# Four graph layers on one core: a planner that counts TensorE's instructions, attention summed by key tile, and checks and turns begun beside the LSTM

## The chip, the cores and the metric

The kernel runs on one core of one Trainium2 chip. Its time is device time in microseconds, the median of three runs. The program is one launch, and its input is packed on the host without arithmetic.

## The reference, cut to what matters

There are 32 graphs of 512 nodes with 128 features each, and one symmetric 0/1 adjacency for each graph. Four layers follow each other. Every one of them normalizes its input, cuts it at zero and adds its result to the residual.

```python
# layer 0: attention over neighbours
v, q, k = relu(h @ Wv.T + bv), relu(h @ Wq.T + bq), relu(h @ Wk.T + bk)
scores = einsum('bih,bjh->bij', q, k)
s = clip(scores * mask, 0.0, CLAMP_HI) - NEG_PENALTY * (1.0 - mask)
x = x + softmax(s, axis=2) @ v

# layer 1: an LSTM over the last 128 nodes makes weights of each graph
dyn = conv1d(h[:, -128:, :]) + conv_b
lw = lstm(dyn)                                # 128 steps, one after the other
x = x + sigmoid((A_norm @ h) @ lw)            # A_norm = D^-1/2 (A + I) D^-1/2

# layer 2: four times
src_agg = (adj / rownorm) @ (nodes @ ws + bs)
dst_agg = (adj.T / colnorm) @ (nodes @ wd + bd)
out = tanh(concat([src_agg, nodes @ wn + bn, dst_agg]) @ wu + bu)

# layer 3
g = adj @ (h @ W.T) + bias
x = x + where(g >= 0, g, a * g)
```

## The kernel before

The program has three stages. In the first (`pass_1`, one call for each batch) it computes keys, values and the attention of a batch's last 128 nodes, which is all that the LSTM needs, and stores keys, queries and values in DRAM.

In the second stage the LSTM runs. It handles all 32 batches in one step, so there are 128 steps in a row. A step goes from TensorE (`f_z`, L1234) to ScalarE (`f_th`, L1260), VectorE (`f_cu`, L1266, and `f_th`, L1267), ScalarE (`f_tcn`, L1274), VectorE (`f_h`, L1278, and a transpose into `f_seq`, L1279), and back to TensorE. Beside it runs `pass_2`: for each batch the attention of the first 384 nodes. For each of four key tiles there is a product of scores (`f_s`, L1325), an exponential (`f_e`, L1328) and a product with the mask (L1329). Then the values are summed (`f_po`, L1334): for each of three query tiles over the four key tiles. All these products, like those of the LSTM, are cut into four quarters of 32 columns (`quarters`); the planner calls such work tiled and counts a switch to other work as 0.28 or 0.1 us. For batches 0 to 21 (`EARLY`), `pass_2` also makes layer 1's neighbour sums (`f_pg`, L1419) and stores them. Batches 26 and 27 (`FIRST`) keep their adjacency `a`, its squared copy `ar` and their rows in SBUF, so that their later turns begin without loads. Batches 28 to 31 come late (`LATE`).

In the third stage (`rest`) each batch takes a turn: layer 1's end (`f_pl`, L1477), the four layers of layer 2 (`f_py` L1523, `f_pa` L1419 for the sums over neighbours and L1534 for a node's own part, `f_y` L1402 and L1403, the scaling of `f_pa` by the degrees at L1530, `f_n` L1538), and layer 3. The order of turns is 26, 27, then 0 to 25, then 28 to 31.

Each turn also checks that the adjacency equals its transpose, because the program uses that. GpSimd writes `ar` to DRAM as bf16 (`f_das`, L1491), a transposing transfer issued by SyncE brings it back turned (`f_aT`, L1493), and VectorE compares it with `a` in two passes (`f_junk`, L1496), with the count in `viol`. If a check had failed, a general program would run instead.

What stands where is decided by a planner in the kernel (`Plan.run`). Each operation has a rank, the time that it is expected to take, the tiles that it reads and writes, and a gap by which its result comes later. The planner plays the program through. At each step it takes the operation that can start first, by rank among those ready, and reserves buffers (`BUFS`) and PSUM banks. Ranks below 1000 are the LSTM's. Ranks from 20,000 are `pass_2`, ranks from 30,000 (`plan.last`) are `rest`, and the first two turns' main work is moved up beside the LSTM by `SOON`. The instructions are then issued on each engine in the order of the planned start times. Each engine works through its list in order. `hold_back` ties a load that belongs beside the LSTM to an LSTM step on VectorE that ends before its planned start, so that it is not issued earlier.

Of the kernel before, what the change touches and what calls it, by code (L numbers as in the profile page):

```python
# [8 lines left out]
FP = mybir.dt.float32  # L9
# [4 lines left out]
P = 128  # L14
# [503 lines left out]
class Op:  # L518
    __slots__ = ("engines", "rank", "no", "deps", "cells", "waits", "ready", "end", "engine", "start", "next", "gap", "tiled", "patience")


class Plan:
# [14 lines left out]
    SWITCH = (0.28, 0.1)  # L537

# [30 lines left out]
    def op(self, engines, rank, reads=(), writes=(), after=(), gap=0.0, tiled=False):  # L569

        o = Op()
        o.engines, o.rank, o.no, o.gap = engines, rank, len(self.ops), gap
        o.tiled = tiled
        o.patience = 0.15
        deps = set(after)
        cells = []
        for acc, is_write in [(a, False) for a in reads] + [(a, True) for a in writes]:
            c, part = acc if isinstance(acc, tuple) else (acc, None)
            if c not in cells:
                cells.append(c)  # L580
            for key, (ws, rs) in c.parts.items():
                if part is None or key is None or key == part:
                    deps.update(ws)
                    if is_write:
                        deps.update(rs)
            mine = c.parts.setdefault(part, ([], []))
            if is_write:
                c.parts[part] = ([o], [])
            else:
                mine[1].append(o)  # L590
        deps.discard(o)
        o.deps = list(deps)
        o.cells = [c for c in cells if c.pool is not None]
        for c in o.cells:
            c.left += 1
        self.ops.append(o)
        return o

    def hold_back(self, tc, made, o, steps):

        while len(steps) > 1 and steps[1][0] + self.ACROSS["SP"] < o.start:
            steps.pop(0)
        if self.spared <= o.rank < self.last and steps[0][0] + self.ACROSS["SP"] < o.start:
            tc.add_manual_dep(made.ins, steps[0][1].name, mybir.DependencyInfo(
                mybir.DependencyClass.Sync, mybir.DependencyReason.DATA), reason="issued in step with the LSTM")

    def run(self, tc, queues):
# [89 lines left out]
        tiled = False  # L697
        by_rank = sorted((o for o in ops if o.rank >= 10_000 and o not in apart), key=lambda o: -o.rank)
        while done < len(ops):
            best = None  # L700
            for e, cands in pools.items():
                first = None
                held = expected.get(e)
                for rank, no, o in cands:
                    r = room(o)
                    if r is None:
                        continue
                    if r:
                        r += self.HOP
                    s = max(free[e], o.ready[e], r)  # L710
                    if e == "PE" and o.tiled != tiled and rank >= self.spared:
                        s = max(s, free[e] + self.SWITCH[o.tiled])
                    if len(o.engines) > 1:
                        mine = s + o.engines[e][0]
                        if any(max(free[x], o.ready[x], r) + o.engines[x][0] < mine - 1e-9 for x in o.engines if x != e):
                            continue
                    if rank < self.URGENT:
                        held = s
                    elif held is not None and s < held < s + o.engines[e][0] - o.patience:
                        continue  # L720
# [14 lines left out]
            if e == "PE":  # L735
                tiled = o.tiled
            if o.rank < self.URGENT:
                foresee(o)
# [23 lines left out]
        steps = []  # L762
        with tc.manual_schedule(engines=queues):
# [8 lines left out]
def symmetric(ctx, tc, x, adj, weights, cols, rows, lstm_b, prelu_a, out, fail):  # L772
# [20 lines left out]
    FIRST = [B - LATE - 2 + k for k in range(2)]  # L793
    EARLY = range(22)
# [104 lines left out]
    viol = const.tile([P, B, 2], FP, name="f_viol")  # L899
# [320 lines left out]
    def lstm():  # L1220
# [20 lines left out]
        PE(2_000, MANY * T_STEP, lambda z=z: first(z), [], [z], after=conv_ops, tiled=True)  # L1241
        coming, after_th = z, None
        for t in range(T):
# [11 lines left out]
            if t or coming is not None:  # L1255
                ahead = 0.0 if coming is None else T_STEP
                PE(R, ahead + (T_STEP if t else 0.0), step, [], ([z] if t else []) + ([coming] if coming else []),
                   after=last, gap=-ahead, tiled=True)
# [30 lines left out]
    def pass_2(b):  # L1289
# [26 lines left out]
        PE(R, t_mm(NR), lambda: quarters(lambda p: nc.tensor.matmul(pq.t[p], w[:, W_Q, p], hT.t, start=True, stop=True)), [hT], [pq], tiled=True)  # L1316
# [5 lines left out]
        es = []  # L1322
        for j in range(NT):
            s = bank(f"f_s_{b}_{j}", (P, NR), whole=False)
            PE(R, t_mm(NR), lambda s=s, j=j: quarters(lambda p: nc.tensor.matmul(  # L1325
                s.t[p], keys.t[:, j * P + p.start : j * P + p.stop], q.t, start=True, stop=True)), [keys, q], [s], tiled=True)
# [3 lines left out]
            es.append(e)  # L1330
        po = bank(f"f_po_{b}", (P, L, P + 1), whole=False)
        for t in range(L):
            for j in range(NT):
                PE(R, t_mm(P), lambda t=t, j=j: quarters(lambda p: nc.tensor.matmul(  # L1334
                    po.t[p, t, :], es[j].t[:, t * P + p.start : t * P + p.stop], v.t[:, j, :], start=(j == 0), stop=(j == NT - 1))),
                    [es[j], v], [po], tiled=True)
# [5 lines left out]
        if whole and not early:  # L1342
            begun[b] = a, xc, ar, deg
        else:
# [23 lines left out]
    def squares(rank, b, a, name):  # L1368
# [6 lines left out]
        return ar, deg  # L1375

# [38 lines left out]
    def aggregate(rank, parts, ar, pg):  # L1415
# [9 lines left out]
        if rank < plan_rest:  # L1425
            last = PE(rank, 8 * t_r(N), both, [parts, ar], [pg])
# [6 lines left out]
    def rest(b, turn, lw_after):  # L1433
# [54 lines left out]


        das = plan.fixed(dram.tile([N, N], BF, tag=f"s{b}", name=f"f_das_{b}"))  # L1490
        POOL(R + 2, 1.4, lambda: nc.gpsimd.dma_start(das.t.rearrange("(t p) j -> p t j", p=P), f32(ar.t)), [ar], [das], gap=6.0)  # L1491
        aT = new("y", (P, NT, N), f"f_aT_{b}", BF)
        plan.op({"SP": (3.0, lambda: nc.sync.dma_start_transpose(out=aT.t, in_=das.t))}, R + 2, [das], [aT], gap=4.0)  # L1493
        for k in range(2):
            def differ(k=k):
                nc.vector.scalar_tensor_tensor(junk, flat(a.t[:, 2 * k : 2 * k + 2, :]), 1.0, flat(aT.t[:, 2 * k : 2 * k + 2, :]),  # L1496
                                               OP.mult, OP.not_equal, accum_out=viol[:, b, k : k + 1])
            differ_ops.append(DVE(R + 2, 1.2, differ, [a, aT], []))


# [91 lines left out]
    def counted():  # L1592
# [10 lines left out]
        def places():  # L1603
            nc.vector.tensor_reduce(bad[:, 1:2], flat(viol), AX.X, OP.add)
# [11 lines left out]
    sum_ops, differ_ops, late = [], [], []  # L1616
# [8 lines left out]
    for k, b in enumerate(FIRST + [b for b in range(B) if b not in FIRST]):  # L1625
        rest(b, k, end)
# [87 lines left out]
```

## Time and profile before

| what | us |
|---|---|
| median of 3 runs | 1301.07 |
| lowest, highest | 1301.03, 1301.52 |
| the profiled execution | 1305.92 |
| span of its profile, first to last instruction | 1304.0 |
| first `f_z` product to last | 181.8 to 503.3 |
| share of the chain that ended last that is TensorE's | 85% |

The profile is of one execution, and its span is a little shorter than the time, which also has the start and the end of the launch. "Idle before" a group of instructions is time in which their engine did nothing just before them, with what ended it; "issue" means that no other engine's signal ended it. The profile records each fp32 product as two matmuls with a weight load each.

This is the share of the chain by line. The attention's products and the LSTM's stand on it as well as the graph layers':

```profile
PE f_pa L1419 17%; PE f_py L1523 14%; PE f_pa L1534 14%; PE f_pg L1419 8%; PE f_po L1334 5%; PE f_s L1325 5%; PE f_z L1234 4%; PE f_pk L1141 2%; PE f_pol L1184 2%; PE f_pv L1157 2%; PE f_p L1575 2%; PE f_sl L1174 2%; PE f_pl L1477 2%; PE f_pd L1209 2%; PE f_pq L1316 1%
```

### The profile page before, as it was taken

How to read it: one execution, taken by the hardware profiler on the slowest of the kernel's cores; microseconds unless marked ns; L12 is line 12 of the kernel's file. 1: busy time of each engine (PE TensorE's matmuls, PEld its weight loads, DVE VectorE, ACT ScalarE, POOL GpSimd, SP SyncE). 2: the span in 40 equal slices, each digit the busy share in tenths (PEclk: the TensorE clock that was granted, in tenths of full speed). 3: DMA queues.
4: the chain of work that ended last, by engine and by line, in shares of the span. 5: the costliest groups of instructions: out<-in, count | busy, mean ns of one | idle time of the engine just before them, and what ended most of it. 6: DMA issues, size and time to landing. Idle time of an engine off the chain costs nothing.

```text
span 1304.0 us, 32965 instructions
## 1 busy us (share of the span) xinstructions
PE 1268.1 (97%) x12087; PEld 976.6 (75%) x12087; DVE 990.3 (76%) x3284; ACT 830.2 (64%) x2079; POOL 389.8 (30%) x733
## 2 busy tenths in 40 slices
PE   9999999998999999899999999999999999999997
PEld 6888876666766677677778787787777877877774
DVE  7989878877978787587667677676776787787754
ACT  5666667777777554577566676666766665675423
POOL 4654533222222133232213223132231322332000
PEclk9999999999999999899999999999999999999998
DMA  8888888887746655889476667666676366673311
GB/s 259 270 275 285 265 271 273 257 262 252 246 140 215 209 182 139 198 191 243 103 152 156 155 163 163 154 159 154 162 160 144 86 136 145 139 170 65 50 33 35
DMA packets 300699, 232.03 MB, mean 178 GB/s; under 512 B 140656, under 2 KB 246128, under 8 KB 300528
## 3 DMA queue, kind: packets, MB, share of 16 engines
q1 hardware_dynamic: 283632, 213.06, 58.4%
q0 software_dynamic: 16896, 16.78, 8.4%
q8 instruction: 97, 1.59, 0.5%
q14 instruction: 74, 0.61, 0.2%
HBM read 136.19 MB, written 62.13 MB: 152 GB/s over the span
## 4 chain that ended last, share of the span: by engine, by line
PE 85%; DVE 5%; DMA 3%; ACT 2%; issue 2%; POOL 1%; SPq 0%; ACTq 0%; DVEq 0%
PE f_pa L1419 17%; PE f_py L1523 14%; PE f_pa L1534 14%; PE f_pg L1419 8%; PE f_po L1334 5%; PE f_s L1325 5%; PE f_z L1234 4%; PE f_pk L1141 2%; PE f_pol L1184 2%; PE f_pv L1157 2%; PE f_p L1575 2%; PE f_sl L1174 2%; PE f_pl L1477 2%; PE f_pd L1209 2%; PE f_pq L1316 1%
## 5 line engine op out<-in xcount | busy, mean ns | idle before, releaser
L1419 PE MATMUL f_pa<-f_ar,f_y 128*128 128x512 f32 x1024 | 295.6, 426 | 0.7 <-ACT f_y L1402 0.7
L1419 PEld LDWEIGHTS f_pa<-f_ar,f_y 128*128 128x128 f32 x1024 | 189.4, 188 | 72.1 <-issue 37.3
L1523 PE MATMUL f_py<-f_wf,f_n 128*128 128x128 f32 x1280 | 175.0, 276 | 0.0
L1523 PEld LDWEIGHTS f_py<-f_wf,f_n 128*128 128x128 f32 x1280 | 165.4, 192 | 9.3 <-ACT f_n L1538 1.4
L1534 PE MATMUL f_pa<-f_n,f_wf 128*128 128x512 f32 x320 | 153.0, 593 | 0.3 <-DVE f_pa L1530 0.3
L1538 ACT ACTIVATE f_n<-f_pa,f_bcol 128x512 f32<-128x512 f32 x128 | 88.3, 690 | 93.5 <-PE f_pa L1534 93.4
L1373 ACT ACTIVATE f_ar<-f_a 128x512 fp32r<-128x512 f32 x216 | 133.6, 621 | 5.3 <-PE f_pg L1419 3.1
L1402 ACT CAST f_y<-f_py 128x512 fp32r<-128x512 f32 x128 | 74.7, 584 | 93.7 <-PE f_py L1523 88.4
L1491 POOL DMA_DIRECT2D f_das<-f_ar x32 | 27.8, 868 | 354.0 <-ACT f_ar L1373 284.5
L1334 PE MATMUL f_po<-f_v,f_e 128*32 128x129 f32 x3072 | 106.3, 274 | 6.0 <-issue 5.9
L1334 PEld LDWEIGHTS f_po<-f_v,f_e 128*32 128x32 f32 x3072 | 89.3, 110 | 20.4 <-issue 13.2
L1403 DVE TENSOR_TENSOR f_y<-f_py,f_y 128x512 fp32r<-128x512 f32 x128 | 87.4, 686 | 22.0 <-ACT f_y L1402 21.8
L1325 PE MATMUL f_s<-f_q,f_k 128*32 128x384 f32 x1024 | 100.6, 490 | 0.0
L1530 DVE TENSOR_TENSOR f_pa<-f_pa,f_inv 128x512 f32<-128x512 f32 x128 | 86.6, 693 | 16.5 <-PE f_pa L1419 16.1
L1234 PE MATMUL f_z<-f_w,f_seq 128*32 128x128 f32 x2040 | 85.1, 277 | 10.6 <-DVE f_seq L1279 4.2
L1534 PEld LDWEIGHTS f_pa<-f_n,f_wf 128*128 128x128 f32 x320 | 57.9, 190 | 47.1 <-issue 37.7
L1234 PEld LDWEIGHTS f_z<-f_w,f_seq 128*32 128x32 f32 x2040 | 55.4, 109 | 48.1 <-issue 11.4
L1496 DVE SCALAR_TENSOR_TENSOR f_junk<-f_a,f_aT 128x1024 bf16<-128x1024 f32 x64 | 78.1, 1221 | 7.1 <-DMA f_aT<-f_das 6.1
L1419 PE MATMUL f_pg<-f_ar,f_xp_d 128*128 128x512 f32 x256 | 75.3, 417 | 0.3 <-DVE f_xp_d L1411 0.2
L1523 PE MATMUL f_py<-f_wf,f_T_c 128*128 128x128 f32 x448 | 72.9, 275 | 0.0
L1328 ACT ACTIVATE f_e<-f_s 128x384 f32<-128x384 f32 x128 | 60.8, 484 | 17.7 <-PE f_s L1325 9.9
L1096 DVE COPY f_hl_d<-f_n 128x1024 uint16<-128x1024 uint16 x28 | 19.4, 694 | 68.8 <-ACT f_n L1538 68.8
(197 smaller groups left out, 2756.8 us busy)
## 6 DMA issues: line engine op xcount, KB each, us to landing
f_a<-in_adj_dram SPq DMA_DIRECT2D x30, 1024.0 KB
f_a<-in_adj_dram SPq DMA_DIRECT2D x96, 256.0 KB
f_das<-f_ar POOLq DMA_DIRECT2D x32, 512.0 KB, 4.8
f_dkq<-f_kh SPq DMA_DIRECT2D x32, 448.0 KB
f_dv<-f_v SPq DMA_DIRECT2D x32, 258.0 KB
f_v<-f_dv SPq DMA_DIRECT2D x32, 258.0 KB
f_x<-in_x_dram SPq DMA_DIRECT2D x32, 256.0 KB
f_al<-in_adj_dram SPq DMA_DIRECT2D x32, 256.0 KB
```

The lines of the kernel that those rows point to most:

```text
L1234: nc.tensor.matmul(z.t[part, k, :, :], h, w[:, m : m + 4, part], start=False, stop=True, skip_group_check=True)
L1325: PE(R, t_mm(NR), lambda s=s, j=j: quarters(lambda p: nc.tensor.matmul(s.t[p], keys.t[:, j * P + p.start : j * P + p.stop], q.t, start=Tru ...
L1334: PE(R, t_mm(P), lambda t=t, j=j: quarters(lambda p: nc.tensor.matmul(po.t[p, t, :], es[j].t[:, t * P + p.start : t * P + p.stop], v.t[:, ...
L1373: ACT(rank, 0.62, lambda t=t: nc.scalar.activation(ar.t[:, t, :], a.t[:, t, :], AF.Square, accum_out=deg.t[:, t : t + 1]), [(a, t)], [(ar, ...
L1402: ACT(rank, t_act(N), lambda: nc.scalar.copy(parts.t[:, :, 0, :], src.t), [src], [(parts, 0)])
L1403: DVE(rank, t_dve(N), lambda: nc.vector.tensor_sub(parts.t[:, :, 1, :], src.t, f32(parts.t[:, :, 0, :])), [src, (parts, 0)], [(parts, 1)])
L1419: nc.tensor.matmul(pg.t, parts.t[:, j, k, :], ar.t[:, j, :], start=(k == 0 and j == 0), stop=(k == 1 and j == NT - 1))
L1496: nc.vector.scalar_tensor_tensor(junk, flat(a.t[:, 2 * k : 2 * k + 2, :]), 1.0, flat(aT.t[:, 2 * k : 2 * k + 2, :]), OP.mult, OP.not_equal ...
L1523: nc.tensor.matmul(py.t[:, j, :], nodes[n].t[:, bass.ts(j, P)], wf[:, W_F[i] + c, 0, :], start=False, stop=(c == nch - 1), skip_group_chec ...
L1530: before = DVE(R, t_dve(N), lambda pa=pa: nc.vector.tensor_mul(pa.t, pa.t, inv_row.t), [inv_row], [pa])
L1534: nc.tensor.matmul(pa.t, wf[:, W_F[i] + c, 1, :], nodes[n].t, start=False, stop=(c == nch - 1), skip_group_check=True)
L1538: ACT(R, 0.57, lambda pa=pa, n=n, i=i: nc.scalar.activation(n.t, pa.t, AF.Tanh, bias=bcol[:, i : i + 1]), [pa], [n])
```

## The change

It has four parts.

1. The planner counts TensorE's instructions. Each operation gets a `count`, 8 if nothing is said. `supplied` gives the time from which TensorE can have an operation's instructions: 5 us (`FETCH`) after the instruction that stands 264 (`AHEAD`) before them was taken, and 32 (`KEEP`) fewer are available to work that is not the LSTM's while the LSTM runs. Nothing waits in the program for this; it alters which operation is chosen next.
2. Attention in `pass_2` adds to `f_po` as soon as a key tile's weights are there: for each key tile over the three query tiles, where it was for each query tile over the key tiles. One `start` flag is set for the bank, on the first of these products.
3. The check becomes a function, `turned_back`. For batches 26 and 27 it is called in `pass_2`, beside the LSTM, with VectorE's part in four pieces of one tile each. For the others it stays in the turn with two pieces.
4. Batches 22 and 23 (`NEXT`) take the third and fourth turn. Their adjacency is loaded in four pieces. `hold_back` now covers every load planned to start before the LSTM's end, those of later ranks too.

```diff
+    AHEAD, FETCH, KEEP = 264, 5.0, 32
...
-        if self.spared <= o.rank < self.last and steps[0][0] + self.ACROSS["SP"] < o.start:
+        if self.spared <= o.rank and o.start < self.left_at and steps[0][0] + self.ACROSS["SP"] < o.start:
...
+        taken, at_time = [0], [0.0]
+
+        def supplied(o):
+
+            n = taken[-1] + o.count + (self.KEEP if o.rank >= self.URGENT and self.left else 0) - self.AHEAD
+            if n <= 0:
+                return 0.0
+            k = bisect.bisect_left(taken, n)
+            return at_time[k] + self.FETCH - o.engines["PE"][0]
...
-                    if e == "PE" and o.tiled != tiled and rank >= self.spared:
-                        s = max(s, free[e] + self.SWITCH[o.tiled])
+                    if e == "PE":
+                        s = max(s, supplied(o))
+                        if o.tiled != tiled and rank >= self.spared:
+                            s = max(s, free[e] + self.SWITCH[o.tiled])
...
+                taken.append(taken[-1] + o.count)
+                at_time.append(o.end)
...
+        self.left_at = max(o.end for o in order if o.rank < self.URGENT)
...
+    NEXT = [22, 23]
...
-        es = []
+        po = bank(f"f_po_{b}", (P, L, P + 1), whole=False)
         for j in range(NT):
...
-            es.append(e)
-        po = bank(f"f_po_{b}", (P, L, P + 1), whole=False)
-        for t in range(L):
-            for j in range(NT):
-                PE(R, t_mm(P), lambda t=t, j=j: quarters(lambda p: nc.tensor.matmul(
-                    po.t[p, t, :], es[j].t[:, t * P + p.start : t * P + p.stop], v.t[:, j, :], start=(j == 0), stop=(j == NT - 1))),
-                    [es[j], v], [po], tiled=True)
+            for t in range(L):
+                PE(R, t_mm(P), lambda e=e, t=t, j=j: quarters(lambda p: nc.tensor.matmul(
+                    po.t[p, t, :], e.t[:, t * P + p.start : t * P + p.stop], v.t[:, j, :], start=(j == 0 and t == 0),
+                    stop=(j == NT - 1), skip_group_check=True)), [e, v], [po], tiled=True, count=16)
...
         if whole and not early:
             begun[b] = a, xc, ar, deg
+            turned_back(R + 5, b, a, ar, NT)
...
+    def turned_back(rank, b, a, ar, pieces):
+
+        das = plan.fixed(dram.tile([N, N], BF, tag=f"s{b}", name=f"f_das_{b}"))
+        POOL(rank, 1.4, lambda: nc.gpsimd.dma_start(das.t.rearrange("(t p) j -> p t j", p=P), f32(ar.t)), [ar], [das], gap=6.0)
+        aT = new("y", (P, NT, N), f"f_aT_{b}", BF)
+        plan.op({"SP": (3.0, lambda: nc.sync.dma_start_transpose(out=aT.t, in_=das.t))}, rank, [das], [aT], gap=8.0 if b in NEXT else 4.0)
+        n = NT // pieces
+        for k in range(pieces):
+            at = differs[0]
+            differs[0] += 1
+
+            def differ(k=k, at=at):
+                nc.vector.scalar_tensor_tensor(junk[:, : n * N], flat(a.t[:, n * k : n * (k + 1), :]), 1.0, flat(aT.t[:, n * k : n * (k + 1), :]),
+                                               OP.mult, OP.not_equal, accum_out=viol[:, at : at + 1])
+            differ_ops.append(DVE(rank, 0.08 + 0.56 * n, differ, [a, aT], []))
...
-            DMA(R, 1024, lambda: nc.sync.dma_start(a.t, adj[b].rearrange("(t p) j -> p t j", p=P)), [], [a])
+            if b in NEXT:
+                for t in range(NT):
+                    DMA(R, 256, lambda t=t: nc.sync.dma_start(a.t[:, t, :], adj[b, t * P : (t + 1) * P, :]), [], [(a, t)], gap=LANDED)
+            else:
+                DMA(R, 1024, lambda: nc.sync.dma_start(a.t, adj[b].rearrange("(t p) j -> p t j", p=P)), [], [a])
...
+        if b not in begun:
+            turned_back(R + 2, b, a, ar, 2)
...
-    for k, b in enumerate(FIRST + [b for b in range(B) if b not in FIRST]):
+    for k, b in enumerate(FIRST + NEXT + [b for b in range(B) if b not in FIRST + NEXT]):
         rest(b, k, end)
```

Counts of 16 are given to the tiled products and to `f_pg` beside the LSTM, 64 to the LSTM's first products and 16 or 32 to a step's.

More of the change, by code (lines that the diff above doesn't have):

```diff
@@ L518 @@
 class Op:
-    __slots__ = ("engines", "rank", "no", "deps", "cells", "waits", "ready", "end", "engine", "start", "next", "gap", "tiled", "patience")
+    __slots__ = ("engines", "rank", "no", "deps", "cells", "waits", "ready", "end", "engine", "start", "next", "gap", "tiled", "patience", "count")
 class Plan:
@@ L567, in fixed, with op @@
         return c
-    def op(self, engines, rank, reads=(), writes=(), after=(), gap=0.0, tiled=False):
+    def op(self, engines, rank, reads=(), writes=(), after=(), gap=0.0, tiled=False, count=8):
         o = Op()
@@ L574, in op @@
         o.patience = 0.15
+        o.count = count
         deps = set(after)
@@ L898, in symmetric @@
     nc.vector.memset(neg_half, -0.5)
-    viol = const.tile([P, B, 2], FP, name="f_viol")
+    viol = const.tile([P, 2 * B + 2 * len(FIRST)], FP, name="f_viol")
     rinv = const.tile([P, B, NT], FP, name="f_rinv")
@@ L1240, in lstm @@
         z = biased(0)
-        PE(2_000, MANY * T_STEP, lambda z=z: first(z), [], [z], after=conv_ops, tiled=True)
+        PE(2_000, MANY * T_STEP, lambda z=z: first(z), [], [z], after=conv_ops, tiled=True, count=64)
         coming, after_th = z, None
@@ L1257, in lstm @@
                 PE(R, ahead + (T_STEP if t else 0.0), step, [], ([z] if t else []) + ([coming] if coming else []),
-                   after=last, gap=-ahead, tiled=True)
+                   after=last, gap=-ahead, tiled=True, count=16 * ((t > 0) + (coming is not None)))
             th, after_th = after_th or new("th", (P, 5, TURN), f"f_th_{t}"), new("th", (P, 5, TURN), f"f_th_{t + 1}")
@@ L1315, in pass_2 @@
         pq = bank(f"f_pq_{b}", (P, NR), whole=False)
-        PE(R, t_mm(NR), lambda: quarters(lambda p: nc.tensor.matmul(pq.t[p], w[:, W_Q, p], hT.t, start=True, stop=True)), [hT], [pq], tiled=True)
+        PE(R, t_mm(NR), lambda: quarters(lambda p: nc.tensor.matmul(pq.t[p], w[:, W_Q, p], hT.t, start=True, stop=True)), [hT], [pq], tiled=True, count=16)
         q = new("xn", (P, NR), f"f_q_{b}")
@@ L1325, in pass_2 @@
             PE(R, t_mm(NR), lambda s=s, j=j: quarters(lambda p: nc.tensor.matmul(
-                s.t[p], keys.t[:, j * P + p.start : j * P + p.stop], q.t, start=True, stop=True)), [keys, q], [s], tiled=True)
+                s.t[p], keys.t[:, j * P + p.start : j * P + p.stop], q.t, start=True, stop=True)), [keys, q], [s], tiled=True, count=16)
             e = new(f"n{j}" if j < 3 else "y", (P, NR), f"f_e_{b}_{j}")
@@ L1425, in aggregate @@
         if rank < plan_rest:
-            last = PE(rank, 8 * t_r(N), both, [parts, ar], [pg])
+            last = PE(rank, 8 * t_r(N), both, [parts, ar], [pg], count=16)
             last.patience = PATIENCE
@@ L1486, in rest @@
         xn = ln_full(R, xc, f"c2{b}", moved)
[L1490 to L1498, printed above, removed]
+        if b not in begun:
+            turned_back(R + 2, b, a, ar, 2)
         turned_d = new("dt", (P, TURN), f"f_dT_{b}")
@@ L1603, in places @@
         def places():
-            nc.vector.tensor_reduce(bad[:, 1:2], flat(viol), AX.X, OP.add)
+            nc.vector.tensor_reduce(bad[:, 1:2], viol, AX.X, OP.add)
             nc.vector.tensor_add(bad[:, 0:1], bad[:, 0:1], bad[:, 1:2])
@@ L1614, in counted @@
         PE(R, 0.1, read, [], [], after=[said] + late)
-    sum_ops, differ_ops, late = [], [], []
+    sum_ops, differ_ops, late, differs = [], [], [], [0]
     junk = const.tile([P, 2 * N], BF, name="f_junk")
```

## The prediction

> **What bounds the kernel now.** I read the page first (shares of busy time, the slices, the fetch queue), then busy time by stretch with cuts where the stages change, then TensorE's waits, then the timeline at the two places where TensorE is idle longest.
>
> ```profile
> PE 1268.1 (97%) x12087; PEld 976.6 (75%) x12087; DVE 990.3 (76%) x3284; ACT 830.2 (64%) x2079; POOL 389.8 (30%) x733
> ...
> PEclk9999999999999999899999999999999999999998
> ...
> q8 instruction: 97, 1.59, 0.5%
> ```
>
> TensorE is busy for 97% of the span, no other engine over 76%. The stretches (length, busy time of PE, PEld, DVE, ACT and POOL, granted clock, DMA share, GB/s) say where the other 3% is:
>
> ```profile
> 0.00:181.80 181.80, 177.69 (x1420) 148.83 (x1420) 153.74 (x686) 114.87 (x230) 96.41 (x248) 1.00 0.86 272
> 181.80:450.00 268.20, 254.68 (x5190) 176.43 (x5183) 219.51 (x900) 192.78 (x681) 66.78 (x129) 1.00 0.75 234
> 450.00:503.40 53.40, 50.30 (x1204) 38.82 (x1203) 45.67 (x201) 30.91 (x112) 16.55 (x33) 0.97 0.55 172
> 503.40:526.60 23.20, 17.82 (x169) 14.92 (x161) 14.11 (x59) 8.02 (x22) 7.60 (x12) 0.97 0.77 165
> 526.60:540.00 13.40, 13.40 (x59) 9.95 (x60) 7.91 (x14) 9.03 (x22) 2.98 (x5) 0.79 0.69 203
> 540.00:1165.00 625.00, 624.64 (x3382) 489.19 (x3381) 461.96 (x1203) 413.92 (x899) 176.93 (x277) 1.00 0.69 155
> 1165.00:1304.00 139.00, 129.55 (x687) 98.46 (x685) 87.37 (x226) 60.66 (x116) 22.56 (x32) 0.97 0.24 53
> ```
>
> From 540 to 1165 us TensorE lacks 0.36 us: there only less matmul work could help. It is idle 16.6 us beside the LSTM (181.8 to 503.4: 13.5 + 3.1), 5.4 us at the seam after it (503.4 to 526.6), 4.1 us in the first stage and 9.5 us in the last. A lower clock adds 53.4 x 0.03 = 1.6 us and 13.4 x 0.21 = 2.8 us. TensorE's waits (total us, times, longest) name the causes, and the timeline shows the two worst:
>
> ```profile
> PE f_po L1334 <- issue: 5.9, 5, 2.3
> PE f_z L1234 <- DVE f_seq L1279: 4.2, 8, 1.1
> PE f_pa L1534 <- DVE f_sh_c L1076: 3.8, 1, 3.8
> PE f_z L1234 <- ACT f_ar L1373: 2.1, 4, 1.5
> PE f_z L1234 <- issue: 1.5, 2, 1.1
> ```
>
> ```profile
> 470.16 0.94 PE L1334 MATMUL f_po<-f_v,f_e 128*32 128x129 f32 x25
> ...
> 473.37 1.50 PE L1334 MATMUL f_po<-f_v,f_e 128*32 128x129 f32 x36 [2.27 <-issue]
> ...
> 475.55 0.25 ACT L1260 ACTIVATE f_th<-f_z 128x96 f32<-128x96 f32 x1 [4.27 <-PE f_z L1234]
> ```
>
> ```profile
> 524.69 1.22 DVE L1496 SCALAR_TENSOR_TENSOR f_junk<-f_a,f_aT 128x1024 bf16<-128x1024 f32 x1 [3.35 <-DMA f_aT<-f_das]
> ...
> 526.44 0.15 DVE L1076 SCALAR_TENSOR_TENSOR f_sh_c<-f_mv_c,f_rs_c 128x4 f32<-128x4 f32 x1
> ```
>
> ```profile
> 526.59 2.08 PE L1534 MATMUL f_pa<-f_hT_c,f_wf 128*128 128x512 f32 x2 [3.78 <-DVE f_sh_c L1076]
> ```
>
> "Issue" in the midst of one row of like matmuls is a wait for nothing that another engine does: TensorE had no instructions. In the last two (VectorE's, then TensorE's timeline) VectorE stands 3.35 us at the check f_junk, for the turned adjacency; the scaling of f_pa by the degrees, which the next TensorE product needs, stands behind it, and TensorE idles 3.78 us.
>
> [...] 1.59 MB in 97 packets is 16.4 KB each, and TensorE's 2 x 12087 recorded instructions over 97 are 249. [...] 7.4 us (5.9 + 1.5) are waits for issue. [...] here all 32 f_aT are on SyncE's queue and hold it 1.3 to 5.2 us, median 2.25.
>
> **The change, part by part.** The matmuls are the same in number and shape, but for two.
>
> *Fetch.* One block is 128 recorded matmuls and their 128 weight loads. The chain of waits has 72 f_po in 1.99 us, 27.6 ns each: a block of nothing but f_po lasts 3.5 us; with f_s (24 in 1.94 us, 81 ns) it lasts longer. Before the stalls at 352, 445, 461 and 473 us the last 128 matmuls had taken 4.2, 4.3, 3.6 and 3.6 us; before the one at 417 us 6.2, so density is most of the cause, not all. I priced the order in which each built program's TensorE instructions stand with such durations (f_z 27.8 ns, f_pg 229 ns from later rows): of all starting points beside the LSTM the next 264 instructions hold under 4.0 us of work in 8% before and in none after, under 4.75 us in 26% before and 2% after; the least after is 4.5 us. Five LSTM steps before have no other TensorE work between them, none after. So of 7.4 us I take off 6.5, leaving 0.9 (bounds 3 and 7.4), and 1.5 of the 1.6 us of clock after the 2.3 us stall. That attention sums by key tile is what lets f_s and f_po mix in short pieces; its own product count stays 3072 records. It also holds a PSUM bank for f_po from the first key tile on: bounds 0 to +2 us; I take 0, as the LSTM's two f_z banks and this one leave five of eight.
>
> *Marking products.* The two f_marks matmuls beside the LSTM (L963) are not in the new order: 2 x 0.39 = -0.8 us.
>
> *Seam.* The checks of the two batches begun early go from the seam to steps 111 to 118 of VectorE's LSTM order, and four turns instead of two are ready when the LSTM ends. The wait at 524.69 us has no place any more. Of the 5.4 us idle (3.78, 0.92, 0.67) I keep 1.5 us for the first products, which wait for ScalarE and VectorE whichever turn comes first: -3.9; with them goes most of the clock loss, -2.3 of 2.8. Bounds: nothing, and -8.2. What is late next are the checks of batches 22 and 23, whose transfers get more planned time (gap 8 for 4). Each issues a GpSimd write (to landing 4.7 to 8.0 us), a SyncE transpose and two VectorE passes; their 1.22 us passes are hidden as now, since TensorE lacks nothing after 540 us.
>
> *Added beside the LSTM.* Eight check pieces of 512 columns, about half of 1.22 us plus 0.08, some 0.7 each: 5.6 us of VectorE, which is busy 82% there (265.2 of 321.6). A step's own VectorE work stands behind a piece, and TensorE's f_z behind that; other products fill some: +1.0 (0 to +3). Behind the same two waits on f_aT stand LSTM steps, not graph layers (a rival below). The two transposes hold SyncE 2.25 us each; loads queued behind them are due at least 3.8 us ahead: 0 (0 to +1.5). Two adjacencies come in four pieces each, now held to LSTM steps: the DMA share there is 0.75, so 0. Three more f_pg visits: eight f_pg take 2.04 us beside the LSTM and 1.83 us later, so 3 x 0.2 = +0.6.
>
> *Not changed.* f_z waits for other engines 8.2 us (4.2, 2.1 and five small ones); I leave them (bounds -5 and +3). The two extra f_pg of 1.83 us for batches 22 and 23 move from late turns to the seam: 0. The last 90 us of the two TensorE orders are the same row by row, so the tail's 9.5 us stay.
>
> **Sum.** -6.5 - 1.5 - 0.8 - 3.9 - 2.3 + 1.0 + 0.6 = -13.4 us on the profiled execution, 1305.92 us with a span of 1304.0 and 1.9 around it. The runs' median is 1301.07, 4.85 less; some of the waits may be longer under the profiler, so I give back 1.5: -11.9, or **1289.2 us**.
>
> **Rivals.** (1) *The seam's gap is only replaced*: four turns at once want GpSimd's norms (f_dinv L1453 alone 1.72 us each) and the DMA queues, 0.98 and 1.01 busy from 580 to 620 us; TensorE waits for a layer norm as it did for the check. For it: such a wait for f_aT came again at 609 us. Against: there it cost TensorE only 0.34 us. Only fetch and marks count: -6.5 - 1.5 - 0.8 + 1.6 + 1.5 = -5.7, 1295.4. (2) *The evener order also ends the waits of f_z*: fewer steps start late, 8.2 falls to about 3: -17.1, 1284. (3) *The fetch waits are a matter of DMA traffic, not of density* (the stall at 417 us speaks for it, the other four against): the seam alone, -0.8 - 3.9 - 2.3 + 1.6 + 1.5 = -3.9, 1297.2. (4) *Slower: VectorE stands at the checks beside the LSTM*, at steps 111 and 116, until f_aT lands; each us is a us of the LSTM, since every step passes VectorE. The slowest f_das and f_aT here took 8.0 and 8.05 us, 16 together against 14.4 planned (1.4, 6, 3 and 4): 1.7 us a check. It decides from 6 us a check on and is slower by over 0.2% from 7.3; at 8 each, 1301.1 - 11.9 + 16 = 1305.
>
> **How the numbers follow.** Forecast 0.53, (1) 0.22, (2) 0.13, (3) 0.08, (4) 0.04. The forecast's own bounds reach about 1284 to 1295; with (1) and most of (2) the range is 1282 to 1297. No change means within 0.2%, 2.6 us, about what a measurement here can tell: faster is below 1298.5, which takes in all but (4) and some of (3).
>
> **What would show it.** Right: TensorE's waits for issue under 1.5 us in all, clock 1.00 from 450 us to the LSTM's end, the span from the first to the last f_z at 310 to 315 us instead of 321.5, idle under 2 us at the seam, no f_marks product after the start, f_junk's first start before the last f_z. Wrong: issue still above 4 us (3), a new idle of over 3 us soon after the last f_z (1), or a VectorE wait on f_aT of several us among the LSTM's steps (4).

## The result, and the profile after

| | before | after |
|---|---|---|
| median of 6 runs, us | 1302.87 | 1289.8 |
| lowest, highest | 1301.03, 1305.94 | 1287.1, 1293.02 |
| the profiled execution, its span | 1305.92, 1304.0 | 1290.13, 1288.3 |
| first to last `f_z` product | 181.8 to 503.3 | 179.0 to 495.9 |

The ratio of after to before is 0.9901, interval 0.9878 to 0.9923: faster by 1.0%. Of the six runs of before, three are those of the table above (1301.0 to 1301.5 us); the three taken beside after took 1304.2 to 1305.9. The page of after, with the same lines as the prediction showed of before:

```profile
PE 1259.9 (98%) x12085; PEld 971.5 (75%) x12085; DVE 985.2 (76%) x3279; ACT 834.1 (65%) x2092; POOL 386.9 (30%) x733
...
PEclk9999999999999999999999999999999999999999
...
q8 instruction: 97, 1.59, 0.5%
```

The clock row shows no dip any more. Busy time by stretch of after (length, busy PE, PEld, DVE, ACT, POOL, granted clock, DMA share, GB/s), cut where its own stages change:

```profile
0.00:179.00 179.00, 173.86 (x1380) 147.33 (x1384) 150.77 (x672) 113.66 (x226) 94.74 (x245) 1.00 0.87 272
179.00:450.00 271.00, 259.10 (x5289) 181.16 (x5283) 224.24 (x925) 201.88 (x715) 69.24 (x136) 1.00 0.77 242
450.00:495.90 45.90, 44.38 (x969) 30.95 (x961) 40.28 (x172) 30.45 (x110) 15.38 (x33) 1.00 0.86 241
495.90:520.00 24.10, 23.91 (x348) 20.97 (x346) 22.53 (x92) 15.77 (x45) 14.11 (x22) 1.00 0.68 150
520.00:540.00 20.00, 19.91 (x143) 15.24 (x142) 17.04 (x45) 16.02 (x36) 5.84 (x11) 1.00 0.92 216
540.00:1150.00 610.00, 610.00 (x3307) 477.65 (x3306) 444.13 (x1152) 395.46 (x849) 167.50 (x258) 1.00 0.69 150
1150.00:1288.30 138.30, 128.75 (x684) 98.16 (x682) 86.22 (x225) 60.86 (x116) 20.06 (x31) 0.98 0.23 53
```

Read as length less PE busy: beside the LSTM TensorE is idle 11.9 + 1.5 = 13.4 us (16.6 before), at the seam after it 0.19 + 0.09 = 0.3 us (5.4 before), at a clock of 1.00 where before had 0.79. The last stretch has its 9.5 us still. What remains beside the LSTM, by TensorE's waits (total us, times, longest), and the longest wait for issue in the timeline:

```profile
PE f_z L1252 <- issue: 5.0, 3, 2.0
PE f_z L1252 <- DVE f_seq L1297: 2.9, 7, 1.1
PE f_z L1252 <- ACT f_ar L1389: 2.1, 4, 1.5
```

```profile
408.91 0.61 PE L1252 MATMUL f_z<-f_w,f_seq 128*32 128x128 f32 x14
411.48 0.27 PE L1252 MATMUL f_z<-f_w,f_seq 128*32 128x128 f32 x1 [1.95 <-issue]
```

The reader is to see two things. The wait for a layer norm at the seam is gone from the list. The waits for issue are not: they fell from 7.4 us to 5.0 (three waits), and now they stand within a row of `f_z`, on the LSTM's own path, where the profile shows no other engine late.

The span fell by 15.7 us. Idle time gives 35.9 - 28.4 = 7.5 of it: 3.2 beside the LSTM and 5.1 at the seam, with 1.0 more in the first stage and small changes elsewhere. Busy time gives 8.2: 4.4 were the lower clock (1.6 + 2.8, as the prediction worked them out), 0.8 the two marking products, and 3.0 are spread over many groups and not assigned.

### The profile page after: what moved, and what is told of

Read it like the earlier page. It is cut to its first block, busy times and chain, and to the rows that moved or that the text cites. A ratio compares the mean times of both kernels' runs of the same rounds, so it can differ in the third digit from the quotient of the medians.

```text
span 1288.3 us, 33017 instructions
## 1 busy us (share of the span) xinstructions
PE 1259.9 (98%) x12085; PEld 971.5 (75%) x12085; DVE 985.2 (76%) x3279; ACT 834.1 (65%) x2092; POOL 386.9 (30%) x733
## 4 chain that ended last, share of the span: by engine, by line
PE 86%; DVE 7%; ACT 2%; DMA 2%; POOL 1%; issue 1%; DVEq 0%; ACTq 0%; SPq 0%; POOLq 0%
PE f_pa L1451 18%; PE f_py L1548 15%; PE f_pa L1559 15%; PE f_pg L1451 8%; PE f_s L1343 5%; PE f_z L1252 4%; PE f_po L1349 4%; PE f_p L1600 2%; PE f_pk L1159 2%; PE f_pv L1175 2%; PE f_pl L1513 2%; PE f_pol L1202 2%; PE f_sl L1192 2%; PE f_pd L1227 1%; PE f_pq L1334 1%
## 5 line engine op out<-in xcount | busy, mean ns | idle before, releaser
L1451 PE MATMUL f_pa<-f_ar,f_y 128*128 128x512 f32 x1024 | 299.3, 429 | 0.0
L1252 PE MATMUL f_z<-f_w,f_seq 128*32 128x128 f32 x2040 | 83.6, 276 | 12.6 <-issue 5.0
L1252 PEld LDWEIGHTS f_z<-f_w,f_seq 128*32 128x32 f32 x2040 | 53.0, 109 | 48.7 <-issue 16.4
L1405 DVE SCALAR_TENSOR_TENSOR f_junk<-f_a,f_aT 128x1024 bf16<-128x1024 f32 (+1 forms) x68 | 78.5, 1154 | 4.7 <-DMA f_aT<-f_das 3.7
L1114 DVE COPY f_hl_d<-f_n 128x1024 uint16<-128x1024 uint16 x28 | 19.4, 693 | 75.9 <-ACT f_n L1563 75.9
L1086 ACT ACTIVATE f_xn_c<-f_x,f_sh_c,f_rs_c 128x128 f32<-128x128 f32 x140 | 59.1, 486 | 18.9 <-DVE f_sh_c L1094 18.5
```

Of the source, the lines that this page charges most:

```text
L1252: nc.tensor.matmul(z.t[part, k, :, :], h, w[:, m : m + 4, part], start=False, stop=True, skip_group_check=True)
L1405: nc.vector.scalar_tensor_tensor(junk[:, : n * N], flat(a.t[:, n * k : n * (k + 1), :]), 1.0, flat(aT.t[:, n * k : n * (k + 1), :]), OP.mu ...
L1451: nc.tensor.matmul(pg.t, parts.t[:, j, k, :], ar.t[:, j, :], start=(k == 0 and j == 0), stop=(k == 1 and j == NT - 1))
```

## The experiments

A kernel with one part undone is also planned anew, and the order of everything beside the LSTM changes with it. So each run was read twice: by its ratio to before, and by two stages of its trace. The table is the summary. The measured times of e1, e2, e3, e5, e6 and e7 lie outside every band that their expectations had set, so the traces, not the totals, carry what follows. The idle times are length less PE busy; "issue + f_seq" is the sum of TensorE's waits for these two from 170 to 520 us (to 600 in e9 to e12).

| kernel | us | ratio to before (95%) | idle beside LSTM | issue + f_seq | idle in the 60 us after last f_z |
|---|---|---|---|---|---|
| before | 1302.87 | 1 | 16.6 | 7.4 + 4.2 | 5.4 |
| after | 1289.8 | 0.9901 (0.9878, 0.9923) | 13.4 | 5.0 + 2.9 | 0.3 |
| e1 no counting | 1299.91 | 0.9968 (0.9952, 0.9984) | 17.7 | 3.8 + 7.0 | 1.4 |
| e2 checks back | 1319.09 | 1.0104 (1.007, 1.0138) | 11.8 | 4.4 + 3.7 | 6.0 |
| e3 no NEXT | 1299.38 | 0.9942 (0.9917, 0.9966) | 15.0 | 4.7 + 2.7 | 3.4 |
| e4 old sum | 1290.53 | 0.9886 (0.9849, 0.9922) | 12.9 | 0.2 + 7.2 | 0.3 |
| e5 two checks left out | 1298.94 | 0.9957 (0.9936, 0.9977) | 11.0 | 2.5 + 4.7 | 3.3 |
| e6 counting and sum only | 1308.34 | 1.0031 (1.0019, 1.0043) | 12.7 | 5.7 + 2.5 | 7.7 |
| e7 seam parts only | 1304.12 | 0.9985 (0.9967, 1.0003) | 24.8 | 8.6 + 10.8 | 2.9 |
| e9 e7, two comparisons left out | 1301.05 | 0.9983 (0.9962, 1.0003) | 18.0 | 6.9 + 5.1 | 0.5 |
| e10 old hold_back | 1291.86 | 0.9899 (0.988, 0.9917) | 14.3 | 5.3 + 3.0 | 0.1 |
| e11 refill 4.8 us | 1291.46 | 0.9908 (0.9883, 0.9934) | 12.7 | 2.5 + 6.5 | 0.8 |
| e12 refill 5.2 us | 1300.1 | 0.9957 (0.9942, 0.9973) | 15.0 | 1.4 + 9.0 | 2.8 |

**The scale of what a total can tell: e11 and e12.** They differ from after, and from each other, in one number of the planner.

```diff
-    AHEAD, FETCH, KEEP = 264, 5.0, 32
+    AHEAD, FETCH, KEEP = 264, 4.8, 32      (e12: 5.2)
```

> The changed kernel with the planner's refill time 4.8 us instead of 5.0: a control. The order beside the LSTM is drawn anew, the work packed there is nearly the same (1.5 us more before the last f_z, by my pricing of the order), 9.7% instead of 4.9% of the starting points have under 5 us of work. If differences of 8 to 18 us between the variants are effects of the parts they leave out, this one stays within 1287 to 1293. If any new plan scatters the time by as much, it falls outside 1284 to 1296. Waits for issue 3 to 6 us.

> The changed kernel with 5.2 us instead of 5.0: the second control, to the other side (8.8% of the starting points under 5 us, work beside the LSTM within 1.3 us). Same reading: 1287 to 1293 if a new plan alone does little, outside 1284 to 1296 if the variants before were read from scatter. In the micro run the dense phase beside loads took 5.5 us a block of 256 on average and up to 8, so 5.2 should not end the waits for issue either: 3 to 6 us.

e11 came out as the changed kernel does. e12's 1300.1 lies outside 1284 to 1296, which its expectation had set down as the mark of scatter. TensorE's waits in e12:

```profile
PE f_z L1252 <- DVE f_seq L1297: 9.0, 15, 2.8
PE f_py L1548 <- ACT f_py L985: 2.3, 1, 2.3
```

So a new plan with the same parts can cost some 10 us. Between the two profiles 4.4 us of it are idle time (32.8 us in e12, 28.4 in after), and 5.6 are longer busy time, in part at a lower clock (0.89 from 527.3 to 542.3 us, around the wait for `f_py`). No variant's total that lies within 10 us of after prices the part it leaves out, and those of e1, e3 and e5 do; only a wait or a stage that follows the part can. Waits for issue don't follow the planner's refill time: they are 2.5, 5.0 and 1.4 us at 4.8, 5.0 and 5.2 us, beside 6.5, 2.9 and 9.0 us for `f_seq`.

**Counting: e1 and e4.** e1 drops the planner's line that delays a TensorE operation until its instructions can be there. e4 puts back the old loop of sums over query tiles and keeps the counting.

```diff
-                        s = max(s, supplied(o))
```

```diff
-            for t in range(L):
-                PE(R, t_mm(P), lambda e=e, t=t, j=j: ...
+        for t in range(L):
+            for j in range(NT):
+                PE(R, t_mm(P), lambda t=t, j=j: ...
```

> The changed kernel without the planner's use of the instruction supply; all else stays. By instruction counts 27% of the starting points beside the LSTM then have under 5 us of work in the next 264 instructions, 5% with it and 32% in the kernel before. Theory D (TensorE's waits for instructions are set by how dense the order is): waits for issue of 6 to 8 us in all (5.0 in the changed kernel), one or more of over 2 us in the midst of f_po, time about 1294 to 1296 us. Theory T (they are set by how long a fetch takes under the DMA traffic, wherever it falls): issue stays near 5 us and the time within 1.5 us of the changed kernel's, 1289 to 1291.

> The changed kernel with attention summed query tile by query tile as before; supply counting, checks and begun turns stay. By counts the order is nearly as even (6% under 5 us of work in 264 instructions, least 4.1 against 4.5). If the summing order is only a means to evenness that the counting finds anyway: within 2 us of the changed kernel, 1288 to 1292. If it is what lets the counting work: waits for issue back at 6 us or more and 1293 to 1296.

e4 is as fast as after: the new order of summing is worth nothing that the runs can tell. e1 is slower. By label it has fewer waits for issue than after (3.8 us against 5.0), and its `f_z` waits longer for `f_seq`. But its list has one more wait that seems to belong with issue:

```profile
PE f_z L1251 <- DVE f_seq L1296: 7.0, 20, 1.5
PE f_z L1251 <- issue: 2.9, 2, 1.8
PE f_wT L1031 <- DMA f_a<-in_adj_dram: 2.3, 1, 2.3
```

`f_wT` does not read `f_a`. Its own weights had landed by 281.5 us, and its first weight load ran at 291.9 us; the product behind it came at 294.2. The wait follows 128 recorded products in quarters. All seven waits for issue in before end 2.2 to 2.6 us after a 16 KB packet of TensorE's instruction queue (q8 on the page) began, and all three in after 2.2 to 2.5 us after one; the two longest waits of before for `f_seq`, 1.06 and 1.09 us, end 6.7 and 7.3 us after one. That `f_wT`'s wait is one for instructions too is the author's estimate, from the label that doesn't fit and the row ahead of it. With it e1 waits 6.1 us for instructions, within the 6 to 8 us of theory D.

What counting does shows in the work ahead of these waits, taken as the time in which the last 128 matmuls started. In before it is 3.5 to 5.1 us at six of the seven waits, and 6.2 at the one at 417 us; ahead of e1's `f_wT` it is 3.5 us. In the nine kernels that count, no wait for issue of over 0.3 us has less than 5.6 us ahead of it. Counting thus ended the waits behind dense rows, which were its target. What is left in after follows looser rows, at 184, 351 and 411 us, and e2, e3, e6 and e10 have waits within 4 us of the same places.

By the columns of the table, the nine kernels that count are idle 11.0 to 15.0 us beside the LSTM, the four that do not 16.6 to 24.8, and issue plus `f_seq` is 7.2 to 10.4 us against 10.8 to 19.4 (13.1 for e1 with the wait of `f_wT`). The share of the two labels moves from plan to plan more than their sum. By these groups counting is worth about 4 us of idle time there.

**The refill by itself: e8.** A kernel of nothing but products in quarters of 32 columns, like the LSTM's, in four stretches: 129 columns wide (3200 recorded matmuls) and 384 wide (1600), first without loads, then each beside a row of 1 MB loads of the adjacency. It computes none of the reference and ran once.

```python
for phase, (n, count, loads) in enumerate(((129, 400, 0), (384, 200, 0), (129, 400, 1), (384, 200, 1))):
    ...
    for k in range(count):
        quarter_mm(nc, acc, w, gate, n)
```

> None of the reference's work: four phases of quarter-wide fp32 products alone on TensorE, 129 columns (a block of 256 instructions lasts 3.5 us) and 384 columns (10.3 us), first without other transfers, then the same two beside a constant stream of 1 MB loads on SyncE's queue. Theory D (density decides): the 129-column phases wait for instructions with and without loads, the 384-column ones in neither. Theory T (the fetch's turnaround under traffic decides): the first 129-column phase has no wait of over 0.3 us, the third has one at nearly every block, 1 to 3 us each (400 groups of 16 instructions are 25 blocks), the 384-column phase beside loads has none or few since 10 us cover a turnaround of 4 to 9 us.

Busy time of the four stretches (length, busy PE, PEld, DVE, POOL, clock, DMA share, GB/s), then TensorE's timeline without loads and with them:

```profile
3.00:103.00 100.00, 94.70 (x3200) 89.10 (x3192) 0.07 (x1) 0.00 (x0) 1.00 0.32 89
104.00:232.00 128.00, 128.00 (x1592) 51.61 (x1588) 0.16 (x1) 0.00 (x0) 1.00 0.01 2
234.00:371.00 137.00, 101.62 (x3183) 96.74 (x3179) 0.52 (x2) 0.00 (x0) 0.93 0.85 309
373.00:501.00 128.00, 128.00 (x1592) 62.51 (x1588) 0.45 (x1) 0.00 (x0) 1.00 0.90 329
```

```profile
63.34 3.72 PE L43 MATMUL g_acc<-g_gate,g_w 128*32 128x129 f32 x128 [0.28 <-issue]
67.34 7.45 PE L43 MATMUL g_acc<-g_gate,g_w 128*32 128x129 f32 x256 [0.28 <-issue]
```

```profile
294.59 5.39 PE L43 MATMUL g_acc<-g_gate,g_w 128*32 128x129 f32 x128 [2.47 <-issue]
300.78 3.73 PE L43 MATMUL g_acc<-g_gate,g_w 128*32 128x129 f32 x128 [0.80 <-issue]
307.25 3.73 PE L43 MATMUL g_acc<-g_gate,g_w 128*32 128x129 f32 x128 [2.74 <-issue]
313.45 3.73 PE L43 MATMUL g_acc<-g_gate,g_w 128*32 128x129 f32 x128 [2.47 <-issue]
```

Beside the loads TensorE stops after every 128 recorded matmuls; in the first timeline it stops after 128 or runs on through 256. With their weight loads 128 matmuls are 256 recorded instructions, called a block here; in before the 97 packets of q8, 16.4 KB each, come to 249 recorded instructions a packet. Without loads a block comes every 4.0 us or a little sooner (63.34 to 67.34 is 4.0; the work alone takes 3.7), and TensorE waits 5.0 us in 100. Beside the loads it comes every 6.2 to 6.5 us (the starts of the second timeline), and TensorE waits 35.4 us in 137, of which the loads fill the first 111. The wide products, 1592 in 128.0 us or some 10 us a block, never wait for issue, with loads or without. This is close to what theory T forecast. So in e8 the waits of up to 2.74 us took both, a dense row and loads: here the forecast's density and rival 3's traffic act together. The planner's 5.0 us lies between the two refill times.

A busy DMA is not enough, though. The first stretch is quiet only from about 37 us on; before that the kernel's 8.4 MB of output are written. The page has both kinds of traffic, in slices of 12.6 us:

```profile
DMA  6970000000000000002999999995029999999950
GB/s 192 286 224 5 4 4 4 5 3 1 1 3 1 1 1 1 3 1 90 383 386 386 385 385 385 385 385 193 4 79 383 387 387 386 387 386 386 386 187 1
```

Beside the writes, at 286 GB/s and a DMA share of 0.9 or more from 12.6 to 25.2 us, TensorE never waited over 0.8 us for issue: that is the longest of the whole first stretch, so by estimate a block of 3.7 us never took more than some 4.5. Beside the loads, at 385 GB/s, it took 6.2 to 6.5. Which difference decides, the direction or the rate, was not varied, and where in the refill the loads' time goes was not shown.

**The seam: e2, e3, e6, e5.** e2 puts the checks of batches 26 and 27 back into their turns. e3 empties `NEXT`. e6 does both. e5 leaves out the checks of these two batches, with their transfers.

```diff
-            turned_back(R + 5, b, a, ar, NT)
...
-        if b not in begun:
-            turned_back(R + 2, b, a, ar, 2)
+        turned_back(R + 2, b, a, ar, 2)
```

```diff
-    NEXT = [22, 23]
+    NEXT = []
```

> The changed kernel with the two early batches' checks in their own turns again, two pieces each, behind the LSTM; supply counting, summing order and the two begun turns stay. If the check at the seam was what TensorE lost there: VectorE waits 2 to 4 us for f_aT soon after the last f_z, TensorE idles 2 to 5 us there and the clock drops below 0.95 in that stretch, time 1294 to 1297 us. If the two turns begun beside the LSTM are what covers the seam: TensorE idles under 1 us there, with or without VectorE's wait, time 1289 to 1291.

> The changed kernel with the old order of turns (26, 27, 0, 1, ...), the checks beside the LSTM kept. If the begun turns cover the seam: TensorE idles 2 to 5 us after the last f_z and the time is 1293 to 1296. If moving the checks was enough: idle under 1.5 us there and 1289 to 1291.5.

> The changed kernel with both seam parts undone: the checks back in their turns and the old order of turns; supply counting and the new summing order stay. Theory B: without the two begun turns nothing waits for the two tiles in a hurry, so the 1319 us of checks alone put back must fall to about the kernel before less what the counting brings beside the LSTM: 1294 to 1300. If the checks cost at the seam by themselves, it stays above 1310.

> The changed kernel with the checks of batches 26 and 27 left out altogether (their symmetry is then not looked at, and 60 of 64 check counts stay). The two tiles of adjacency that the 26th and 27th hold come free without a check, as early as in the changed kernel or earlier, and the loads for batches 22 and 23 can be issued beside the LSTM. Theory B (putting the checks back cost 29 us because they held those two tiles, so that the next two turns' loads were issued at 523.6 us instead of 461.6): no wait on f_py of 8 us, those loads before 480 us, time 1287 to 1291. Theory W (the check's own wait on VectorE and its transfers at the seam made the loss): also fast, but by the missing work alone, 1284 to 1288, and the loads' issue doesn't matter. If both fall: near 1319.

In e2 the wait of before is back. VectorE's and SyncE's timeline of e2, then SyncE's of after:

```profile
520.29 1.23 DVE L1404 SCALAR_TENSOR_TENSOR f_junk<-f_a,f_aT 128x1024 bf16<-128x1024 f32 x1 [3.03 <-DMA f_aT<-f_das]
...
523.62 4.43 SPq L1474 DMA_DIRECT2D f_a<-in_adj_dram  x8
```

```profile
461.60 1.39 SPq L1475 DMA_DIRECT2D f_a<-in_adj_dram  x2
...
475.68 3.43 SPq L1475 DMA_DIRECT2D f_a<-in_adj_dram  x4
```

In e5's timeline the last pieces of these two adjacencies, and in before's the next two adjacencies, are issued so:

```profile
458.40 0.91 SPq L1474 DMA_DIRECT2D f_a<-in_adj_dram  x2
```

```profile
528.14 3.40 SPq L1441 DMA_DIRECT2D f_a<-in_adj_dram  x2
```

Two tiles hold a whole adjacency (`BUFS` gives tag `a` two), and batches 26 and 27 keep theirs until they are compared. In after that is done from 457.6 us on, and the adjacencies of 22 and 23 are loaded beside the LSTM; in e2 they are asked for at 523.6 us, after batch 26's comparison, when the turns of 26 and 27 are under way with little else beside them. So it was in before, at 528.1 us. TensorE in e2 waits at the seam (6.0 us, at a clock of 0.70 from 508 to 536 us) and once more for 8.6 us, at 590 us, when the turns of 26 and 27 have ended and those of 22 and 23 stand at the start of layer 2:

```profile
PE f_py L1546 <- ACT f_T_c L1113: 8.6, 1, 8.6
```

The late loads are the cause that the order of events suggests. TensorE's list may be another: it takes up half of batch 22's sums, and all of 23's, only from 564 us on, though the squares for them were made by 540 us. Of the 31.2 us between the profiles of e2 and after, 16.8 are idle time and 14.4 longer busy time, at a mean clock of 0.985 against 0.998. In e5, where no comparison holds the two tiles, all pieces were issued by 459.3 us and no wait for `f_py` was over 0.5 us: both marks of theory B came in, its time did not.

e6 issues its next adjacency at 523.75 us in the same way as e2, and idles 7.7 us. e3, with the checks early and no `NEXT`, idles 3.4 us, the longest being 1.7 us for `f_py`. e6, for which a gain was expected, came out slower than before, and e5, with less work than after, slower than after. e5's own loss is a late piece of an adjacency: ScalarE waited 3.98 us for `f_a` at 532.7 us, and TensorE 2.2 us behind it. All four thus show gaps in the same 60 us, but e3's and e5's totals are within what e12 lost by its plan alone. What is shown is that the loads go out late in e2 and e6 and early in e5 and after, and that the waits go with them; that the held tiles cause the whole of these waits is argued from the order of events. The price of `NEXT` alone stays open.

**The seam parts without counting: e7 and e9.** e7 is after without the counting and with the old loop of sums. e9 leaves out, of e7, VectorE's comparison of batches 26 and 27.

```diff
-        for k in range(pieces):
+        for k in range(0 if pieces == NT else pieces):
```

> The changed kernel without the supply counting and with the old summing order: the two seam parts and the later reach of the held loads alone. If the parts add: the seam's share, 6 to 9 us less than the kernel before, 1293 to 1297 with before at 1302 to 1304. If they need the counting (as the kernel without it, at 1300, hints): 1299 to 1303.

> The kernel of e7 (early checks and NEXT, no counting, old order of summing) without VectorE's eight check pieces of batches 26 and 27; their f_das writes and f_aT transposes stay, so only the comparison of these two adjacencies is left out. In e7 VectorE stood 7.0 us at the first piece, at 484 us, for a transpose that SyncE had issued at 483.25, and the next f_z waited 6.7 us behind it. If that wait is what made the early checks a loss without counting (rival 4 of the prediction, with its price): TensorE's idle time beside the LSTM falls from 24.8 to 16 to 19 us, no f_z wait over 3 us, 1293 to 1298. If the wait was covered by work that only moves (the time is lost anyway): 1301 to 1305.

e7 has the prediction's rival 4 in its trace. SyncE, VectorE and TensorE in e7's timeline:

```profile
478.91 3.08 SPq L1400 DMA_TRANSPOSE f_aT<-f_das  x1
...
484.16 0.69 DVE L1407 SCALAR_TENSOR_TENSOR f_junk<-f_a,f_aT 128x512 bf16<-128x512 f32 x1 [7.00 <-DMA f_aT<-f_das]
...
484.78 0.19 DVE L1295 SCALAR_TENSOR_TENSOR f_h<-f_th,f_tcn 128x32 f32<-128x32 f32 x1
...
485.27 1.08 PE L1251 MATMUL f_z<-f_w,f_seq 128*32 128x128 f32 x16 [6.74 <-DVE f_seq L1296]
```

VectorE stood 7.0 us at the first piece, the LSTM's `f_h` behind it, and `f_z` 6.74 us behind that. The write of this adjacency had gone out at 456.9 us, but its transpose stood on SyncE's queue behind loads that waited for other transfers, until 478.9 us, and landed at 484.1. (The transpose at 483.25 us, which e9's expectation names, is the second batch's.) In after the transposes left at 448.4 and 455.1 us, and `f_junk` did not wait beside the LSTM. In e9's profile the stand is gone and the idle time is 18.0 us, as its theory had it. The times do not follow: 0.9983 and 0.9985 are the same, and 1301.05 us lies in the second band, for time that is lost anyway. e7's profiled execution (1311.07) was 7 us over its median, so the stand cannot have been as long in its usual run; what it usually costs was not measured.

**hold_back: e10.** The old condition, by rank, in place of the new one, by the LSTM's end. TensorE's order stays as it is; some loads lose a wait.

```diff
-        if self.spared <= o.rank and o.start < self.left_at and steps[0][0] + self.ACROSS["SP"] < o.start:
+        if self.spared <= o.rank < self.last and steps[0][0] + self.ACROSS["SP"] < o.start:
```

> The changed kernel with the old condition in hold_back: loads of ranks above the LSTM's are no longer held to an LSTM step. TensorE's order is the same instruction for instruction; some 25 loads lose a wait. If the new condition keeps loads from crowding the LSTM's own transfers: 1291 to 1296, with longer f_z waits for f_ar or f_seq or more waits for issue. If it only writes down the order that SyncE's queue has anyway: 1288 to 1291.5, no difference.

The median is 0.4 us over one band and inside the other; the ratio, 0.9899, is that of after (0.9901). No difference is shown.

## Why the prediction was right, and where it was wrong

The forecast was 1289.2 us, and after took 1289.8. That they agree so closely is in part luck. The errors of the sum cancel, as the table shows. And the profiled executions differ by 15.8 us, where the sum said 13.4; the forecast took 11.9 from a median of 1301.07, which before did not reach again beside after.

Of the prediction's six signs of being right four came in: the clock, the idle time at the seam, the marking products and the start of `f_junk`. The waits for issue (5.0 us, not under 1.5) and the span of `f_z` (316.9 us, not 310 to 315) did not, and issue above 4 us was its sign for rival 3.

| term of the sum | predicted, us | in the two traces |
|---|---|---|
| waits for issue | -6.5 | -2.4 (7.4 to 5.0) |
| clock beside the LSTM | -1.5 | -1.6 |
| marking products | -0.8 | -0.8 |
| seam, idle | -3.9 | -5.1 (5.4 to 0.3) |
| seam, clock | -2.3 | -2.8 |
| check pieces on VectorE | +1.0 | f_z's waits for other engines 8.2 to 6.0, so no loss is seen |
| three more f_pg visits | +0.6 | not told apart |

**The step that failed is the fetch term.** It took off 6.5 us and got 2.4. Its half on density was right, since the waits behind dense rows are gone. But it judged every place by one refill time, so that "4.5 us at the least" seemed enough. The stall at 417 us, with 6.2 us of work before it, was in the prediction and set aside as one in five. It was the telling one: before the three waits in after the last 128 matmuls had taken 7.2, 6.3 and 5.8 us. From the start of these 128 matmuls to the end of the wait it was 8.9, 8.1 and 8.0 us there and 8.0 us at the stall at 417 us, against 4.2 to 6.2 us at the other six waits of before. So the refill is no fixed number in these kernels. e8 shows that loads alone can lengthen it (from 4.0 us to 6.2 to 6.5), and from the start of the 128 matmuls to the packet the DMA queues moved 296, 306 and 310 GB/s before the three waits, where the stretch to 450 us has 242 on average. But e8's refill never took over 6.5 us (not the 8 of e12's expectation), beside denser loads (385 GB/s). At the three waits the packet began only 5.7 to 6.6 us after the start of the block, and what held it back so long stays open.

Over the whole LSTM of after a 16 KB packet starts every 6.3 us on average (50 of them), so by this estimate no order can put 8 us of work in every block. That a plan can still come through almost without waits for issue is shown by e4 (0.2 us).

**Rival 2 supplied part of what was lost.** The waits of `f_z` for other engines fell too, by 2.2 us, and over the 13 kernels those that count are less idle beside the LSTM, while issue and `f_seq` trade places. The forecast held the one fixed while it took off the other. The traces show no common cause of the two, so why they trade places stays open.

**The seam went as described, and further.** The 1.5 us left for the first products was too much, presumably because the four turns' products fill each other's waits. What the prediction did not see is why the checks had to go early for `NEXT` to work at all: the two tiles of tag `a`. It named the loads of 22 and 23 only as traffic.

**Rival 4 did not occur in after.** Its condition, a transpose late on SyncE's queue, came about in e7's plan. There the wait passed on to `f_z` almost whole (7.0, then 6.74 us), as it was priced; in the times of e7 and e9 that price is not seen.

**Giving back 1.5 us for the profiler had no ground.** The profiled execution of after, 1290.13 us, lies among its six runs, and the median of before in later runs was 1304.5 to 1305.1 us, near its profiled 1305.92.

The two halves of the change do not add: counting with the new sum alone 1.0031, the seam parts alone 0.9985, both 0.9901. For the first, e2 and e6 point to the held tiles. For the second only e7's profiled stand is there. Either half left out takes back the whole gain: e6 is 18.5 us over after and e7 14.3, against the 10.3 us that e12 lost by its plan alone. By that measure the loss in e6 is clear, and the one in e7 is only somewhat larger than scatter.

## What to carry to other kernels

When an engine waits for issue, measure the refill of its instructions beside the transfers that run there before taking a threshold from other places; a wait with plenty of work ahead of it is the one that tells. Where a label names a tile that the waiting instruction doesn't read, look at what else ends there. Before moving a check or any last reader, ask which buffer it frees and what is queued for that buffer: here the next loads stood behind the check. Where a planner orders the work, vary one indifferent number first; its scatter, here 10 us, is the least that a total must exceed before a part is priced by it.

## What the runs showed of the hardware

- In e8 a block of 128 dense products with their weight loads came every 6.2 to 6.5 us beside 385 GB/s of loads (243.92 to 344.99 us), and TensorE waited up to 2.74 us for each. In quiet a block came every 4.0 us or a little sooner. Beside writes at up to 286 GB/s no wait for issue was over 0.8 us.
- In before and after the last packet of TensorE's instruction queue to begin before a wait for issue ended took 0.9 to 1.1 us, and TensorE went on 2.2 to 2.6 us after its start (ten waits). It began 1.6 to 3.9 us after the start of the last 128 matmuls at six waits of before, 5.5 us at the one at 417 us, and 5.7 to 6.6 us at the three of after.
- In e8, of ten blocks after a wait of 2.47 to 2.74 us, six took 5.1 to 5.4 us and four 3.73 (313.45 us above is one). The granted clock was 0.68 and 0.72 in two of the slow ones (250.4 to 255.7 and 281.9 to 287.0 us) and 1.00 in two blocks of 3.73 us after shorter waits (at 256.9 and 300.8 us). The wait after a slow block was 0.80 to 1.38 us, after the others 2.47 to 2.74 as long as the loads ran. What makes a block slow after one such wait and not after another was not shown.
- In before the granted clock was 0.50 from 474.1 to 477.5 us, just behind the wait of 2.27 us that ended at 473.37, and 0.50 from 525.3 to 532.1 us, around the end of the 3.78 us idle at the seam (526.59). In after it was 1.00 behind each of the three waits for issue, of 1.44 to 1.95 us (184.1 to 187.0, 351.0 to 354.5 and 411.5 to 415.0 us).
